# Transposes of an attention block moved from TensorE to VectorE and DMA, with the feed-forward stage moved into the next batch

## The chip, the cores and the metric

The kernel runs on one core of a Trainium2 chip. The metric is the device time of one execution in microseconds (us), as a median over timed runs. One further execution is recorded by the hardware profiler; the rows shown below come from it.

## The reference

Four batches of 1024 tokens with 512 channels, all in float32. Each batch has six vectors of modulation from a small condition. The attention has 16 heads, but the same scores for every head (`head_f` is all ones), and the feed-forward stage is a sum over eight square factors, so that both reduce to plain products.

```python
mod = (_silu(L0_c) @ L0_wmod).reshape(L0_c.shape[0], 6, 1, -1)
sa, ca, ga, sb, cb, gb = (mod[:, 0], ..., mod[:, 5])
ga = (2 * (ga >= 0) - 1) * jnp.maximum(jnp.abs(ga), 0.25)   # gb likewise
h = _layernorm(x, axis=-1) * (1 + ca) + sa
x = x + ga * attention(h, Wq, Wk, Wv, Wo)
h = _layernorm(x, axis=-1) * (1 + cb) + sb
x = x + gb * ffn(h, factors, bias)

# attention: qf = h @ Wq.T, kf = h @ Wk.T (rank 64)
scores = jnp.einsum('hr,bir,bjr->bhij', head_f, qf, kf)
attn = softmax(scores)
out = attn @ (h @ Wv.T) @ Wo.T          # heads side by side
# ffn: einsum('btd,rde->bte', x, factors) / sqrt(8) + bias
```

## The kernel before

A batch is held as eight tiles `x` of 128 tokens by 512 channels. TensorE contracts over partitions, so what is contracted has to stand with the contracted index on the partitions; that is what the transposes are for. A float32 product of 128x512 is two instructions in the profile.

The stages of a batch are these.

- **First normalization** (`ln1`, L312): statistics of each tile on VectorE, the inverse root by a power on POOL (`rstd_of`, L270), then `xn_a` on VectorE (`normalize`, L281), in two halves of four tiles.
- **Its transpose.** For batch 0 by TensorE (`hT_steps`). For the others by `hT_by_dma` (L326): VectorE transposes each tile in blocks of 32 by 32 into `st` (L335), and 16 SBUF to SBUF transfers per half, issued on the sync queue SP, carry the blocks to their places in `hT_a` (L338). Each moves 64 KB in runs of 512 bytes.
- **Projection** (`project`, L371) to queries and keys, one call per half.
- **Scores and softmax.** `scores(b, p)` (L398) takes a pair of token tiles: the products, the row maximum on VectorE (L417), the exponential on ScalarE (L419), which writes the numerators `pr` and their sums. `transpose_probs(b, p, jp)` (L425) transposes the numerators on TensorE, four 128x128 blocks to a PSUM tile (`ps_pt`, L433), and ScalarE and VectorE copy these by turns to `pt` (L440, L442). The denominators are applied later, in `attn_out`.
- **First product** (`z_steps(b, half)`, L450): `xn_a` transposed times `pt`, for a half of the tokens in eight steps, a column block of 128 channels in two steps; the result goes to `zt` by ScalarE and VectorE by turns (L466, L468).
- **Output product** (`attn_out`, L493): `zt` times the combined weight `w` of the batch (`make_w`); VectorE adds it to `x` (L502) and takes the statistics of the second normalization.
- **Second normalization** (`ln2`, L511): `xn_f`; then eight groups per batch of four TensorE transposes (`ln2_transposes`, `ps_hT_f`, L295), whose results are scaled and shifted to `hT_f` by ScalarE (L302) and VectorE (L306) by turns.
- **Feed-forward** (`ffn`, L529): `hT_f` times the summed factors `f` (`make_f`); VectorE adds it to `x` (L538), SP stores the tile (L539) and loads the tile of the batch after next into the same place (L99).

`sum_factors` (L251) adds the eight factors in batch 0's loop, through three staging buffers filled on SP.

The loop over `b` computes the first product of batch `b` while it prepares projection, scores and softmax of batch `nb = b + 1`. `weave(main, fill)` interleaves two lists of steps by hand. The order on each engine is fixed when the program is built: it follows the source, but an instruction whose operands or buffers are judged to be late is overtaken by later ones. On the chip each engine, and each DMA queue, works its list in order. PSUM has two tiles for scores, two for transposes (`ps_t`) and two for products (`ps_m`). The numerators of a pair and `xn_f` share two buffers (`prp`), `hT_a` and `hT_f` share two (`hp`).

Of the kernel before, what the change touches and what calls it, by code (L numbers as in the profile page):

```python
# [30 lines left out]
def kernel(  # L31
# [17 lines left out]
    nc = tc.nc  # L49
# [6 lines left out]
    GT = NT // 2  # L56
    GW = GT * P
    EPS = 1e-5
    PSUM = bass.MemoryType.PSUM
# [15 lines left out]
    ps_s = ctx.enter_context(tc.tile_pool(name="ps_s", bufs=2, space=PSUM))  # L75
    ps_t = ctx.enter_context(tc.tile_pool(name="ps_t", bufs=2, space=PSUM))
    ps_m = ctx.enter_context(tc.tile_pool(name="ps_m", bufs=2, space=PSUM))

    def psum_mm(name):
        return ps_m.tile([P, 512], F32, tag="mm", name=name)  # L80

    def psum_tr(name):
        return ps_t.tile([P, 512], F32, tag="tr", name=name)

# [92 lines left out]
    def channels(rows, name, plus):  # L177

        ps = psum_tr(f"ps_ch_{name}")
        for kc in range(KC):  # L180
            nc.tensor.transpose(ps[:, ts(kc, B)], rows[:, ts(kc, P)], ident[0:B, 0:B])
        m = const.tile([P, KC, B], F32, name=f"mod_{name}")
        nc.vector.tensor_scalar(
            m.rearrange("p k b -> p (k b)"), ps[:, : KC * B], plus, None, ALU.add
        )
        return m
# [26 lines left out]
    def first_rows():  # L213
# [3 lines left out]

        ps = psum_tr("ps_qbias")
        for kc in range(KC):
# [31 lines left out]
    def sum_factors():  # L251
        for kc in range(KC):
            acc = None
            for r in range(NR):
                f = stg.tile([P, D], F32, tag="stg", name=f"factor_{kc}_{r}")
                nc.sync.dma_start(out=f, in_=factors[r, ts(kc, P), :])
                if r > 0:
                    nc.vector.tensor_tensor(fsum[:, kc, :], acc, f, ALU.add)  # L258
                acc = f if r == 0 else fsum[:, kc, :]
# [18 lines left out]
    def normalize(b, tiles, mv, xn, name):  # L278
        r = rstd_of(mv, tiles, name)
        for j, t in enumerate(tiles):  # L280
            nc.vector.tensor_scalar(  # L281
                xn[:, j, :], xt[b, t], mv[:, t, 0:1], r[:, j : j + 1],
                ALU.subtract, ALU.mult,
            )
# [5 lines left out]
    def transpose_group(xn, hT, kc, name, scale=None, shift=None):  # L290


        ps = psum_tr(f"ps_hT_{name}_{kc}")
        for j in range(GT):
# [26 lines left out]
    def add_c1(b):  # L321
        bc = spread("c1", b)
        for t in range(NT):
            nc.vector.tensor_tensor(xt[b, t], xt[b, t], bc, ALU.add)

    def hT_by_dma(b, g):  # L326

        Q = 32
        st = stp.tile([P, KC, P // Q, GT, Q], F32, tag="st", name=f"st_a_{b}_{g}")
        hT = hp.tile([P, KC, GW], F32, tag="hT", name=f"hT_a_{b}_{g}")
        for t in range(GT):
            nc.vector.transpose(st[:, :, :, t, :], xn1[b, g][:, t, :])  # L335
        for k in range(P // Q):
            for c in range(P // Q):
                nc.sync.dma_start(  # L338
                    out=hT[ts(c, Q), :, ts(k, GT * Q)], in_=st[ts(k, Q), :, c, :, :]
                )  # L340
        return hT
# [50 lines left out]

    def qk_steps(b, hT):
        return [lambda g=g: project(b, g, hT[g]) for g in range(2)]

    probs, rinv, PT = {}, {}, {}

    def scores(b, p):  # L398
# [14 lines left out]
        den = small.tile([P, 2], F32, tag="den", name=f"den_{b}_{p}")  # L413
        pr2 = prp.tile([P, 2, T], F32, tag="pr", name=f"pr_{b}_{p}")
        for k, (i, ps) in enumerate(pss):
            nm = small.tile([P, 1], F32, tag="nm", name=f"nm_{b}_{i}")
            nc.vector.tensor_reduce(nm, ps, AX.X, ALU.max, negate=True)  # L417
            pr = pr2[:, k, :]
            nc.scalar.activation(  # L419
                pr, ps, AF.Exp, bias=nm, scale=1.0, accum_out=den[:, k : k + 1]  # L420
            )
            probs[b, i] = pr
        nc.vector.reciprocal(rinv[b][:, 2 * p : 2 * p + 2], den)

    def transpose_probs(b, p, jp):  # L425

        half, off = divmod(2 * p, GT)
        if (b, half) not in PT:
            PT[b, half] = ptp.tile([P, NT, GW], F32, tag="pt", name=f"pt_{b}_{half}")
        ps = psum_tr(f"ps_pt_{b}_{p}_{jp}")  # L430
        for jj in range(2):
            for k in range(2):
                nc.tensor.transpose(  # L433
                    ps[:, ds((2 * jj + k) * P, P)],
                    probs[b, 2 * p + k][:, ts(2 * jp + jj, P)], ident,
                )
        dst = PT[b, half][:, ts(jp, 2), ds(off * P, 2 * P)]
        src = ps.rearrange("p (j i) -> p j i", j=2)
        if jp % 2 == 0:
            nc.scalar.copy(dst, src)  # L440
        else:
            nc.vector.tensor_copy(dst, src)  # L442

    def softmax_steps(b, p, nxt):
        steps = [] if nxt is None else [lambda: scores(b, nxt)]
        return steps + [lambda jp=jp: transpose_probs(b, p, jp) for jp in range(NT // 2)]

    ZT = {}

    def z_steps(b, half):  # L450
# [5 lines left out]
        def part(dc, jh):  # L456
# [7 lines left out]
            if jh == 1:  # L464
                if dc % 2 == 0:
                    nc.scalar.copy(zt[:, dc, :], hold[dc])  # L466
                else:
                    nc.vector.tensor_copy(zt[:, dc, :], hold[dc])  # L468

# [40 lines left out]

    def ln2(b, g):  # L511
        if g == 0:
            bias_b[b] = spread("gbias", b)
        xn = prp.tile([P, GT, D], F32, tag="pr", name=f"xn_f_{b}_{g}")
        xn2[b, g] = normalize(b, halves(g), mv2[b], xn, f"f_{b}_{g}")
        hT2[b, g] = hp.tile([P, KC, GW], F32, tag="hT", name=f"hT_f_{b}_{g}")
        for t in halves(g):
            nc.vector.tensor_tensor(xt[b, t], xt[b, t], bias_b[b], ALU.add)  # L518
# [40 lines left out]
    scores(0, 0)  # L559
    for p in range(NT // 2):  # L560
        for step in softmax_steps(0, p, p + 1 if p + 1 < NT // 2 else None):
            step()
        if p == 0:
            second_rows()
    add_c1(0)
    make_w(0)


    for b in range(B):
        nb = b + 1 if b + 1 < B else None  # L570
        if nb is not None:
            hTn = []
            for g in range(2):
                ln1(nb, g)
                hTn.append(hT_by_dma(nb, g))
            scale_wqk(nb)
        weave(z_steps(b, 0), [] if nb is None else qk_steps(nb, hTn))
        if nb is not None:
            add_c1(nb)
            scores(nb, 0)  # L580
        if b == 0:
            sum_factors()
        make_f(b)
        weave(
            z_steps(b, 1),
            [] if nb is None else softmax_steps(nb, 0, 1) + softmax_steps(nb, 1, 2),
        )
        fill = [] if nb is None else softmax_steps(nb, 2, 3) + softmax_steps(nb, 3, None)
        weave([lambda t=t: attn_out(b, t) for t in halves(0)], fill[:5])
        ln2(b, 0)  # L590
        weave(
            [lambda t=t: attn_out(b, t) for t in halves(1)],
            fill[5:] + ln2_transposes(b, 0),
        )
        if nb is not None:
            make_w(nb)
        ln2(b, 1)
        weave([lambda t=t: ffn(b, t) for t in halves(0)], ln2_transposes(b, 1))
        for t in halves(1):
            ffn(b, t)  # L600

# [32 lines left out]
```

## Time and profile before

| | |
|---|---|
| timed runs | 620.51, 625.64 (median) and 627.34 us |
| profiled execution | 620.23 us, span of its instructions 618.2 us, mean granted TensorE clock 0.992 |
| TensorE, busy | 591.9 us (96%) |
| VectorE, busy | 321.9 us (52%) |
| ScalarE, busy | 93.6 us (15%) |
| POOL, busy | 16.8 us (3%) |
| SP queue | 44.37 MB, 22.7% of the 16 DMA engines' span |
| transposes of numerators, L433 | 256 instructions |
| transposes of the second normalization, L295 | 128 instructions |

The span runs from the first to the last instruction; the profiled execution's own time adds 2.0 us around it. PE is TensorE's matrix multiply, PEld its weight load, DVE VectorE, ACT ScalarE, SPq the sync queue. In a row of the lines view, the operation is followed by the tile it writes and those it reads, their shapes and the count; then the busy time in us and the mean of one in ns; then the idle time of the engine before them and what ended it. Matmuls overlap one another, so that a mean of one is longer than the distance from one to the next.

### The profile page before, as it was taken

Reading aid. Unit: us, or ns where it says so; the run is one execution under the profiler, and the core shown is the slowest. Engines: PE = TensorE matmul, PEld = TensorE weight load, DVE = VectorE, ACT = ScalarE, POOL = GpSimd, SP = SyncE. Lnnn points to the kernel's source line nnn. Section 1 sums busy time; section 2 is a strip of 40 time slices with the busy share of each in tenths; the row PEclk is TensorE's granted clock in tenths of the full one; section 3 lists DMA queues with packets and bytes.
Section 4 is the critical chain, followed back from the end, with each engine's and each line's share of the span. In section 5 each row is a group of like instructions: output and inputs, shape, how many; then the busy total and the mean of one; then the engine's idle time right before and its main releaser. Section 6 shows DMA issues by size and latency. Waiting matters only on the chain.

```text
span 618.2 us, 4783 instructions
## 1 busy us (share of the span) xinstructions
PE 591.9 (96%) x1744; PEld 272.2 (44%) x1744; DVE 321.9 (52%) x586; ACT 93.6 (15%) x154; POOL 16.8 (3%) x22
## 2 busy tenths in 40 slices
PE   6898949999999999999999999999999999999997
PEld 3343514344455444344454444344454444444443
DVE  5459993775578584332578584222578220005651
ACT  0223401222211001222211001222211000000110
POOL 1000000000000000000000000000000000000000
PEclk9999988999999999999999999999999999999999
DMA  8950135553001453000001453000001200000011
GB/s 310 381 193 0 37 102 138 186 170 103 0 0 51 154 161 91 21 0 1 0 0 52 154 160 99 12 0 1 0 1 35 101 35 0 1 0 1 0 68 69
DMA packets 35391, 44.67 MB, mean 72 GB/s; under 512 B 4116, under 2 KB 16916, under 8 KB 35368
## 3 DMA queue, kind: packets, MB, share of 16 engines
q1 hardware_dynamic: 35368, 44.37, 22.7%
q8 instruction: 14, 0.23, 0.2%
q14 instruction: 9, 0.07, 0.0%
HBM read 29.64 MB, written 8.42 MB: 62 GB/s over the span
## 4 chain that ended last, share of the span: by engine, by line
PE 80%; DVE 14%; SPq 2%; POOL 2%; issue 1%; DMA 1%; ACT 0%; POOLq 0%; ACTq 0%
PE ps_z L460 34%; PE ps_f L533 14%; PE ps_o L497 14%; PE ps_sc L408 5%; PE ps_qk L371 5%; PE ps_pt L433 3%; DVE xn_f L281 2%; PE ps_hT_f L295 2%; DVE w L481 2%; SPq L338 1%; DVE x L502 1%; DVE x L518 1%; POOL r_f L270 1%; DVE bn_a L275 1%; DVE xn_a L281 1%
## 5 line engine op out<-in xcount | busy, mean ns | idle before, releaser
L460 PE MATMUL ps_z<-pt,xn_a 128*128 128x512 f32 x512 | 227.2, 595 | 0.0
L460 PEld LDWEIGHTS ps_z<-pt,xn_a 128*128 128x128 f32 x512 | 94.7, 190 | 116.2 <-issue 114.0
L497 PE MATMUL ps_o<-w,zt 128*128 128x512 f32 x256 | 114.9, 594 | 0.0
L533 PE MATMUL ps_f<-f,hT_f 128*128 128x512 f32 x256 | 113.3, 592 | 0.0
L533 PEld LDWEIGHTS ps_f<-f,hT_f 128*128 128x128 f32 x256 | 47.2, 191 | 51.5 <-issue 50.0
L497 PEld LDWEIGHTS ps_o<-w,zt 128*128 128x128 f32 x256 | 46.5, 190 | 50.4 <-issue 48.1
L468 DVE COPY zt<-ps_z 128x512 f32<-128x512 f32 x16 | 11.0, 689 | 90.2 <-PE ps_z L460 90.2
L419 ACT ACTIVATE pr<-ps_sc,nm 128x1024 f32<-128x1024 f32 x32 | 35.5, 1113 | 72.0 <-DVE nm L417 72.0
L417 DVE TENSOR_REDUCE nm<-ps_sc 128x1 f32<-128x1024 f32 x32 | 37.8, 1213 | 16.2 <-PE ps_sc L408 16.2
L502 DVE SCALAR_TENSOR_TENSOR x<-ps_o,ri,x 128x512 f32<-128x512 f32 x32 | 23.9, 746 | 41.9 <-PE ps_o L497 41.6
L538 DVE TENSOR_TENSOR x<-ps_f,x 128x512 f32<-128x512 f32 x32 | 21.9, 685 | 40.8 <-PE ps_f L533 40.8
L408 PE MATMUL ps_sc<-kT,qT 64*128 64x512 f32 x128 | 41.1, 617 | 1.6 <-ACT pr L419 1.6
L433 PEld LDWEIGHTS ps_pt<-ident,pr 128*128 128x128 f32 x256 | 30.0, 141 | 27.4 <-issue 18.5
L371 PE MATMUL ps_qk<-hT_a,wqk 128*128 128x512 f32 x64 | 30.3, 621 | 9.9 <-DMA hT_a<-st_a 9.4
L433 PE MATMUL ps_pt<-ident,pr 128*128 128x128 f32 x256 | 36.2, 275 | 1.5 <-ACT pt L440 1.0
L442 DVE COPY pt<-ps_pt 128x512 f32<-128x512 f32 x32 | 21.8, 682 | 21.1 <-PE ps_pt L433 21.0
L440 ACT COPY pt<-ps_pt 128x512 f32<-128x512 f32 x32 | 18.8, 587 | 88.0 <-PE ps_pt L433 87.9
L466 ACT COPY zt<-ps_z 128x512 f32<-128x512 f32 x16 | 9.4, 586 | 131.6 <-PE ps_z L460 131.6
L302 ACT ACTIVATE hT_f<-ps_hT_f,mod_sb,mod_cb 128x512 f32<-128x512 f32 x16 | 12.5, 779 | 103.9 <-PE ps_hT_f L295 88.5
L258 DVE TENSOR_TENSOR fsum<-fsum,factor 128x512 f32<-128x512 f32 x24 | 16.5, 688 | 16.8 <-DMA factor<-in_factors_dram 16.5
L275 DVE BATCH_NORM_STATS2 bn_a<-x 128x6 f32<-128x512 f32 x32 | 21.2, 672 | 7.4 <-DMA x<-in_x_dram 7.4
L408 PEld LDWEIGHTS ps_sc<-kT,qT 64*128 64x128 f32 x128 | 13.8, 186 | 25.1 <-issue 19.4
(82 smaller groups left out, 334.0 us busy)
## 6 DMA issues: line engine op xcount, KB each, us to landing
x<-in_x_dram SPq DMA_DIRECT2D x32, 256.0 KB, 4.1
factor<-in_factors_dram SPq DMA_DIRECT2D x32, 256.0 KB, 3.0
out_dram<-x SPq DMA_DIRECT2D x32, 256.0 KB, 2.0
hT_a<-st_a SPq DMA_DIRECT2D x96, 64.0 KB, 2.0
wm_a<-in_wmod_dram SPq DMA_DIRECT2D x2, 1024.0 KB, 9.5
wm_b<-in_wmod_dram SPq DMA_DIRECT2D x2, 1024.0 KB
wvs<-in_wv_dram SPq DMA_DIRECT2D x4, 256.0 KB
wos<-in_woT_dram SPq DMA_DIRECT2D x4, 256.0 KB, 4.8
```

The lines of the kernel that those rows point to most:

```text
L275: nc.vector.bn_stats(st, src)
L371: nc.tensor.matmul(ps[: 2 * R, :], wqkb[b][:, kc, :], hT[:, kc, :], start=(kc == 0), stop=(kc == KC - 1),)
L408: nc.tensor.matmul(ps[:, ts(h, 512)], qT[h * R : (h + 1) * R, ts(i, P)], kT[h * R : (h + 1) * R, :], start=True, stop=True,)
L417: nc.vector.tensor_reduce(nm, ps, AX.X, ALU.max, negate=True)
L419: nc.scalar.activation(pr, ps, AF.Exp, bias=nm, scale=1.0, accum_out=den[:, k : k + 1])
L433: nc.tensor.transpose(ps[:, ds((2 * jj + k) * P, P)], probs[b, 2 * p + k][:, ts(2 * jp + jj, P)], ident,)
L442: nc.vector.tensor_copy(dst, src)
L460: nc.tensor.matmul(hold[dc], xn1[b, jh][:, j - jh * GT, ts(dc, P)], PT[b, half][:, j, :], start=(j == 0), stop=(j == NT - 1),)
L497: nc.tensor.matmul(ps, ZT[b, half][:, kc, ts(j, P)], wb[b][:, kc, :], start=(kc == 0), stop=(kc == KC - 1),)
L502: nc.vector.scalar_tensor_tensor(xi, ps, rinv[b][:, t : t + 1], xi, ALU.mult, ALU.add)
L533: nc.tensor.matmul(ps, hT2[b, g][:, kc, ts(j, P)], fb[b][:, kc, :], start=(kc == 0), stop=(kc == KC - 1),)
L538: nc.vector.tensor_tensor(xi, ps, xi, ALU.add)
```

## The change

The numerators are transposed by VectorE, in place, in blocks of 32 by 32: one instruction for a pair. The exponential writes them in a layout in which the blocks that go to the same partitions stand together, and `move_blocks` then issues 16 SBUF to SBUF transfers per pair on SP, in runs of 64 numbers (256 bytes). Only pairs 0 and 1 of batch 0 are still transposed by TensorE, and ScalarE makes all copies of these. The tokens of `pt` are then in another order, which the copy to `zt` undoes; all of these copies are on ScalarE.

The second normalization is transposed in the same way, except in the last batch: one VectorE instruction and 16 transfers per half, in runs of 32 numbers (128 bytes). ScalarE then scales and shifts `hT_f` in place.

`ffn` of a batch moves to the next loop, after the first two steps of that batch's first product, and the first normalization of the batch after comes behind it. The projection moves from the first half of the first product to the second, with the softmax pairs 0 to 2; pair 3 goes to `attn_out`. The weight `w` is made in the loop that uses it. PSUM keeps two tiles for scores and has four for products and transposes together. All but the first three factor loads go from SP to POOL's queue.

The diff, cut to its core:

```diff
-    ps_t = ctx.enter_context(tc.tile_pool(name="ps_t", bufs=2, space=PSUM))
-    ps_m = ctx.enter_context(tc.tile_pool(name="ps_m", bufs=2, space=PSUM))
+    ps_m = ctx.enter_context(tc.tile_pool(name="ps_m", bufs=4, space=PSUM))
...
             for r in range(NR):
-                nc.sync.dma_start(out=f, in_=factors[r, ts(kc, P), :])
+                queue = nc.sync if kc == 0 and r < 3 else nc.gpsimd
+                queue.dma_start(out=f, in_=factors[r, ts(kc, P), :])
...
+    def move_blocks(src, dst, width):
+        for r in range(NQ):
+            for c in range(NQ):
+                nc.sync.dma_start(
+                    out=dst[ts(c, Q), :, ts(r, width)], in_=src[ts(r, Q), :, c]
+                )
...
+    def by_dma(b, half):
+        return (b, half) != (0, 0)
...
-        pr2 = prp.tile([P, 2, T], F32, tag="pr", name=f"pr_{b}_{p}")
+        pr2 = prp.tile([P, 2 * T], F32, tag="pr", name=f"pr_{b}_{p}")
+        if by_dma(b, 2 * p // GT):
+            view = pr2.rearrange("p (c k e) -> p k c e", k=2, e=Q)
+        else:
+            view = pr2.rearrange("p (k j) -> p k j", k=2)
...
-    def transpose_probs(b, p, jp):
+    def transpose_probs(b, p):
         half, off = divmod(2 * p, GT)
+        pr2 = probs[b, p][0]
+        nc.vector.transpose(pr2, pr2)
+        move_blocks(
+            pr2.rearrange("p (j c w) -> p j c w", j=NT, c=NQ),
+            pt_tile(b, half)[:, :, ds(off * P, 2 * P)], 2 * Q,
+        )
...
+    def softmax(b, p):
+        scores(b, p)
+        transpose_probs(b, p)
...
             if jh == 1:
-                if dc % 2 == 0:
-                    nc.scalar.copy(zt[:, dc, :], hold[dc])
-                else:
-                    nc.vector.tensor_copy(zt[:, dc, :], hold[dc])
+                dst, src = zt[:, dc, :], hold[dc]
+                if by_dma(b, half):
+                    dst = dst.rearrange("p (h t r a) -> p h r t a", h=2, t=2, r=NQ)
+                    src = src.rearrange("p (h r t a) -> p h r t a", h=2, t=2, r=NQ)
+                nc.scalar.copy(dst, src)
...
     def ln2(b, g):
...
+        if b + 1 == B:
+            xn2[b, g] = normalize(
+                b, halves(g), mv2[b], xn.rearrange("p (t d) -> p t d", t=GT), f"f_{b}_{g}"
+            )
+        else:
+            normalize(
+                b, halves(g), mv2[b],
+                xn.rearrange("p (k t e) -> p t k e", k=KC, t=GT), f"f_{b}_{g}",
+            )
+            nc.vector.transpose(xn, xn)
+            src = xn.rearrange("p (n c a) -> p c n a", c=NQ, a=Q)
+            dst = hT2[b, g].rearrange("p k (t r a) -> p r (k t) a", t=GT, r=NQ)
+            for r in range(NQ):
+                for c in range(NQ):
+                    nc.sync.dma_start(out=dst[ts(c, Q), r], in_=src[ts(r, Q), c])
+            for kc in range(KC):
+                hc = hT2[b, g][:, kc, :]
+                nc.scalar.activation(
+                    hc, hc, AF.Identity, bias=second["sb"][:, kc, b : b + 1],
+                    scale=second["cb1"][:, kc, b : b + 1],
+                )
...
-    for p in range(NT // 2):
-        for step in softmax_steps(0, p, p + 1 if p + 1 < NT // 2 else None):
-            step()
-        if p == 0:
-            second_rows()
-    add_c1(0)
-    make_w(0)
+    scores(0, 1)
+    for jp in range(NT // 2):
+        transpose_probs_pe(0, 0, jp)
+    second_rows()
+    softmax(0, 2)
+    for jp in range(NT // 2):
+        transpose_probs_pe(0, 1, jp)
+    softmax(0, 3)
     for b in range(B):
         nb = b + 1 if b + 1 < B else None
+        z0 = z_steps(b, 0)
+        for step in z0[:2]:
+            step()
+        if b > 0:
+            for t in range(NT):
+                ffn(b - 1, t)
+        hTn = []
         if nb is not None:
-            hTn = []
             for g in range(2):
                 ln1(nb, g)
                 hTn.append(hT_by_dma(nb, g))
             scale_wqk(nb)
-        weave(z_steps(b, 0), [] if nb is None else qk_steps(nb, hTn))
+        for step in z0[2:]:
+            step()
+        add_c1(b)
+        make_w(b)
+        fill = []
         if nb is not None:
-            add_c1(nb)
-            scores(nb, 0)
+            fill = [lambda g=g: project(nb, g, hTn[g]) for g in range(2)]
+            fill += [lambda p=p: softmax(nb, p) for p in range(3)]
+        weave(z_steps(b, 1), fill)
         if b == 0:
             sum_factors()
         make_f(b)
         weave(
-            z_steps(b, 1),
-            [] if nb is None else softmax_steps(nb, 0, 1) + softmax_steps(nb, 1, 2),
-        )
-        fill = [] if nb is None else softmax_steps(nb, 2, 3) + softmax_steps(nb, 3, None)
-        weave([lambda t=t: attn_out(b, t) for t in halves(0)], fill[:5])
+            [lambda t=t: attn_out(b, t) for t in halves(0)],
+            [] if nb is None else [lambda: softmax(nb, 3)],
+        )
         ln2(b, 0)
         weave(
             [lambda t=t: attn_out(b, t) for t in halves(1)],
-            fill[5:] + ln2_transposes(b, 0),
-        )
-        if nb is not None:
-            make_w(nb)
+            ln2_transposes(b, 0) if nb is None else [],
+        )
         ln2(b, 1)
-        weave([lambda t=t: ffn(b, t) for t in halves(0)], ln2_transposes(b, 1))
-        for t in halves(1):
-            ffn(b, t)
+    b = B - 1
+    weave([lambda t=t: ffn(b, t) for t in halves(0)], ln2_transposes(b, 1))
+    for t in halves(1):
+        ffn(b, t)
```

## The prediction

> **What bounds the kernel now.** I read first the busy table and the slices, then one whole loop, then the TensorE timeline inside it, then the sync queue (SP) that would carry the new transfers.
>
> ```profile
> PE 591.9 (96%) x1744; PEld 272.2 (44%) x1744; DVE 321.9 (52%) x586; ACT 93.6 (15%) x154; POOL 16.8 (3%) x22
> ...
> PE   6898949999999999999999999999999999999997
> ```
>
> TensorE works 96% of the span; the gaps lie in the first six slices. So only work taken off TensorE, or those gaps, can pay. One loop of steady state, from one `ps_f` run to the next:
>
> ```profile
> 206.90 13.74 PE ps_f L533 x32
> 220.64 13.73 PE ps_z L460 x32
> ...
> 345.81 13.74 PE ps_f L533 x32
> ```
>
> The period is 345.81 − 206.90 = 138.91 us. Its products cost, by the same chain: 128 of `ps_z` at 13.73 per 32, 54.9; 64 of `ps_o` and 64 of `ps_f` at 3.44 per 8, 27.5 each; two projections 2 x 3.43; four score pairs 4 x 1.92. Sum 124.5. The other 14.4 us are 24 groups of four transposes (16 `ps_pt`, 8 `ps_hT_f`): 0.60 us a group, which the timeline bears out (0.43 for the four, the rest at the changes between kinds):
>
> ```profile
> 285.61 0.60 PE L433 MATMUL ps_pt<-ident,pr 128*128 128x128 f32 x4
> 286.05 3.60 PE L460 MATMUL ps_z<-pt,xn_a 128*128 128x512 f32 x8
> ```
>
> **What goes.** In each of three loops all 24 groups leave TensorE: 43.2 us, less 0.8 a loop for the handovers at the scores that stay: **−40.8**. Ahead of the loops, pairs 2 and 3 of batch 0 lose 8 groups, about 0.5 each: **−4**. The last batch keeps its eight `ps_hT_f` groups. And one large wait loses its place:
>
> ```profile
> L371 PE MATMUL ps_qk<-hT_a,wqk 128*128 128x512 f32 x64 | 30.3, 621 | 9.9 <-DMA hT_a<-st_a 9.4 <-DVE wqk L355 0.5
> ```
>
> These 9.4 us fall in loop 0, where the projection of batch 1 stood after four steps of the first product. It now stands after ten, 20.6 us later: **−9.4**. But SP has 32 new transfers of batch 0 ahead of these; at the rate worked out below the second group lands about 2 us after TensorE asks: **+2**. Without any new wait the sum against the profiled execution is 620.2 − 40.8 − 4 − 9.4 + 2 = 568.
>
> **What VectorE and ScalarE take over.** The block transpose exists already:
>
> ```profile
> 235.54 2.48 DVE L335 STREAM_TRANSPOSE st_a<-xn_a 128x512 f32<-128x512 f32 x4
> ```
>
> A pair of numerators or a half of `xn_f` is four times this tile: 2.5 us, six times a loop, +15. Off VectorE go eight `pt` copies at 0.62, four `hT_f` evictions at 0.75 and four `zt` copies at 0.62: −10.5. Net +4.5 of 74 in a period of 139: hidden under TensorE. ScalarE loses eight copies and gains four `zt` copies and four more scalings, on 22 us of work in 139: hidden too. These costs count only as latency: scores end, the second maximum and exponential follow (reciprocal 2.8 us after the scores, L423 after L408), the transpose 2.5 more; about 5.7 with waits.
>
> **What SP gets, the heart of it.** A pair costs 16 transfers of 64 KB in runs of 256 bytes, a half of the second normalization 16 of 64 KB in runs of 128 bytes. Per loop that is 64 + 32, on top of 32 for `hT_a`. The nearest row is those 32, with runs of 512 bytes:
>
> ```profile
> L338 SPq DMA_DIRECT2D hT_a<-st_a x96: 585/599/1207, 81.2 to 386.3; - x96
> ...
> DMA to landing us min/median/max: 2.0/2.0/3.2
> ```
>
> ```profile
> 238.16 11.27 SPq L338 DMA_DIRECT2D hT_a<-st_a  x16
> ```
>
> One issue takes 0.60 us of the queue, with its gap 0.65; sixteen take 10.4. Loads of 256 KB take 0.33 to 0.34. Does the price grow with the number of runs? Bounds: 0.36 an issue (the load row and a gap) and, in proportion to runs, 1.3 for a pair's and 2.6 for a half's. Against growth stands that `wqk` and `wm_a`, whose sources have four runs a partition (512 in all), are issued in 0.37 and 0.38, hardly above the 0.33 of 128 runs. I take 0.65 for both, and keep a linear price as a rival. The engines behind the queue have room: in the window of the sixteen above their share was 0.37, which is 0.37 x 11.0 / 16 = 0.25 us for one transfer of 8 runs and a completion per engine, 28 ns a run; 17 or 33 records, if none took less, would be 0.48 or 0.92 us. The first lies below the issue, the second above it, by 0.27, or 16 x 0.27 = 4.3 us a half; shorter runs should take less than 28 ns, so I leave it at the issue.
>
> **Where a loop now waits.** Clock from the start of `z_steps(b, 1)`. Pair 0's scores end at 5 x 3.44 + 2 x 3.43 + 1.92 = 26.0, its transposed block is ready at 31.7. From there SP is nearly continuous: pairs 0, 1, 2, 3, then the first half of the second normalization (`ln2(b, 0)`), its row spreads (0.8), then the second half. The last of the first half lands 1.45 after its issue ends, one scaling takes 0.78, semaphores 0.4. TensorE asks for that half (`ffn(b, 0)`) after product, projections, scores, `attn_out` and two steps of the next first product: 27.5 + 6.9 + 7.7 + 27.5 + 6.9 = 76.4. With c1 for a pair's issue and c2 for a half's, the wait is 31.7 + 0.8 + 64 c1 + 16 c2 + 2.6 − 76.4 = 64 c1 + 16 c2 − 41.3. At 0.65 that is **10.7 us a loop**, if TensorE keeps to the source's order. The second half is issued by 10.4 later, while four `ffn` tiles cover 13.8: no wait.
>
> The source's order is not kept where an operand is late:
>
> ```profile
> 254.90 1.98 PE L408 MATMUL ps_sc<-kT,qT 64*128 64x512 f32 x4
> 256.81 1.12 PE L460 MATMUL ps_z<-pt,xn_a 128*128 128x512 f32 x2
> 257.87 1.98 PE L408 MATMUL ps_sc<-kT,qT 64*128 64x512 f32 x4
> ```
>
> Two `ps_z` are put between the scores of one pair while `kT` is copied. Likewise I expect one more column block of `ps_z` (two steps, 6.9 us) ahead of `ffn(b, 0)`; the PSUM pool, now four buffers, still holds the last `attn_out` tiles, so not more. Against this: in loop 0 the projection waited 9.4 us with `ps_z` behind it. I take 10.7 − 6.9 = about **4 us a loop, +12**, with 0 and 10.7 as its ends.
>
> **Edits at nothing, and their cover.** Exponentials of pair 2 wait for the landing of pair 0 (two `pr` buffers): ScalarE stands about 2 us, TensorE has 13.8 us of `attn_out` meanwhile. `ln2(b, 0)`'s normalizations wait likewise for pair 2's landing; behind them on VectorE stand the `attn_out` evictions of tiles 4 to 7, and so the PSUM buffer of the next `ps_z`: up to 3 us of TensorE, inside the wait above. Stores and loads of `ffn` queue behind the second half's transfers, then `hT_a`: they land some 10 us before the projection asks; without that cover every us counts. The three scalings per half that follow the first run faster than TensorE's four products. Factor loads on POOL: 29 issues, which no row shows; between SP's 0.33 and the 1.01 of a power (L270) they are 10 to 29 us of POOL in loop 0, and a power queued behind one that waits for a VectorE sum could hold `hT_a` a few us; the summed factors are wanted only a loop later. I take 0, up to 5.
>
> **A rule against it.** The Trainium skill, "DMA: Bandwidth & Descriptors", Specifications, says transfers of under 512 bytes a descriptor fall below line rate, since the engine reads, modifies and writes. No row here has a short run written from SBUF to SBUF. If each run cost twice the 28 ns above, an issue would be 0.95 and 1.85 us, the wait 64 x 0.95 + 16 x 1.85 − 41.3 = 49 us, and the kernel above 700. The same page ("Why small descriptors are slow (HBM only)") takes SBUF to SBUF out of the penalty for small packets; by that the sum stays as it is.
>
> **Sum.** 568 + 12 = 580 in the terms of the profiled execution. The three timed runs (620.51 to 627.34) have their median 5.4 us above it; I add 5 for a median: **585**. About 1% is what a measurement of this kernel can tell from no change.
>
> **Rivals.**
> Everything hidden (chance 0.17): products enough are put ahead of `ffn`. For it: the `ps_z` rows above; against: the 9.4 us. 568 + 5 = 573.
> Source order, full wait (0.18): 568 + 3 x 10.7 + 5 = 605; with SP's price at 0.70 some 10 us more, 615.
> SP becomes the bound (0.28, the other side): an issue's price grows with the runs in a partition. Load row 0.33, `hT_a` with 4 runs 0.60: 0.0675 a run gives 0.87 for 8 and 1.41 for 16, with gaps 0.92 and 1.46. The first half then waits 64 x 0.92 + 16 x 1.46 − 41.3 = 41, the second 23.4 − 13.8 = 9.6: 50.6 x 3 = 152, so 725; at half that growth 0.79 and 1.06: 26 and 3 a loop, 660. It decides from where 3 waits eat 620 − 568: 17.5 a loop, 0.73 an issue for both. For it: 0.60 against 0.33 is unexplained. Against: `wqk` and `wm_a`.
>
> **Chances and range.** Forecast (573 to 600) 0.32; hidden 0.17; full wait 0.18, of which 0.03 ends within 1%; SP bound 0.28, of which 0.02 within 1%; another mishap of a few tens of us, as in the softmax pairs, 0.05, of which 0.03 within 1% and 0.02 slower. Faster 0.64, same 0.08, slower 0.28. Range 565 to 645, the likeliest case alone 573 to 600.
>
> **What would show it.** Right: no `ps_pt` row but 32 transposes, `ps_hT_f` only in the last batch, periods near 128, SP issues of 0.6 us back to back for some 60 us a loop, the wait of `ps_f` for DMA or ScalarE at 0 to 11 us a loop, the projection's wait near 2. Wrong: issues above 0.73, waits of `ps_z` for `pt` or `ps_sc` for `pr`, or VectorE late in the `attn_out` stage.

## The result and the profile after

The change makes the kernel slower. Its median is 674.3 us (671.8 to 676.7, four runs) against 625.7 (620.5 to 627.3) for the kernel before on the same chip: a ratio of 1.079, 95% interval 1.072 to 1.087. The profiled execution took 676.7 us, its span 674.9. It is the slowest of its four runs, and the profiled execution before (620.2) lies below all four of its own, so the two profiles differ by 56.5 us and the medians by 48.6. From the page, the busy table, TensorE's busy slices and the clock granted to it:

```profile
PE 566.4 (84%) x1424; PEld 244.8 (36%) x1424; DVE 328.5 (49%) x546; ACT 97.2 (14%) x158; POOL 34.6 (5%) x51
...
PE   6989989429992399999992399999991499999997
...
PEclk9988999858996599999997599999996699999999
```

TensorE lost its 320 transposes and 25.5 us of busy time, but its share fell from 96% to 84%. Its slices have four holes, and the clock is low in each. Three holes stand once a loop, ahead of `ps_f`; the first stands in loop 0. The chain that ended last gives the period (start, duration, what):

```profile
229.97 30.65 PE ps_f L582 x64
...
381.50 29.99 PE ps_f L582 x64
```

381.50 − 229.97 = 151.5 us, where 138.9 stood before. The groups of the page name the waits (after the second bar: idle time before the group, and what ended it):

```profile
L582 PE MATMUL ps_f<-f,hT_f 128*128 128x512 f32 x256 | 118.5, 623 | 70.3 <-DMA hT_f<-xn_f 47.2
...
L421 PE MATMUL ps_sc<-kT,qT 64*128 64x512 f32 x128 | 40.8, 675 | 23.4 <-ACT kT L396 21.8
```

The feed-forward waits 70.3 us in three loops, 23.4 each, for its transposed normalization. The scores wait 21.8 us for the keys, all but 0.3 of it in loop 0.

**SyncE's price is what was forecast.** For each line on the queue: issues, then minimum, median and maximum of one in ns:

```profile
L334 SPq DMA_DIRECT2D pt<-pr x224: 585/609/1726, 74.0 to 518.7; - x112
...
L559 SPq DMA_DIRECT2D hT_f<-xn_f x96: 585/627/649, 216.4 to 540.2; - x96
```

0.61 and 0.63 us with 8 and 16 runs a partition, against 0.60 with 4: at this size it does not grow with the runs. But the queue is not continuous. Its timeline in loop 1:

```profile
312.46 55.93 SPq L334 DMA_DIRECT2D pt<-pr  x64
368.49 21.43 SPq L559 DMA_DIRECT2D hT_f<-xn_f  x32
```

64 issues at 0.65 are 41.6 us; these took 55.9. SyncE stood some 14 us for VectorE. The last exponentials of pairs 2 and 3 on ScalarE's timeline, and then VectorE's, show why (in brackets the idle time before an instruction):

```profile
326.58 1.11 ACT L439 ACTIVATE pr<-ps_sc,nm 128x1024 f32<-128x1024 f32 x1
...
342.39 1.10 ACT L439 ACTIVATE pr<-ps_sc,nm 128x1024 f32<-128x1024 f32 x1
```

```profile
335.68 0.75 DVE L529 SCALAR_TENSOR_TENSOR x<-ps_o,ri,x 128x512 f32<-128x512 f32 x1 [1.74 <-PE ps_o L524]
...
337.78 2.31 DVE L448 STREAM_TRANSPOSE pr<-pr 128x2048 f32<-128x2048 f32 x1
...
355.64 2.29 DVE L448 STREAM_TRANSPOSE pr<-pr 128x2048 f32<-128x2048 f32 x1
...
369.98 1.91 DVE L284 TENSOR_SCALAR xn_f<-x,mv,r_f 128x512 f32<-128x512 f32 x4 [5.65 <-DMA pt<-pr]
```

The exponentials of pair 2 end at 327.7, yet its transpose comes at 337.8: on VectorE it stands behind four additions of `attn_out`, each of which waits 1.7 us for TensorE. Pair 3's stands behind the other four and the weight `w`, 12 us after its exponential. The second half of the second normalization waits 5.65 us for a landing, since `xn_f` shares the two `pr` buffers. TensorE's timeline at the end of this:

```profile
351.32 7.03 PE L485 MATMUL ps_z<-pt,xn_a 128*128 128x512 f32 x16
381.50 8.96 PE L582 MATMUL ps_f<-f,hT_f 128*128 128x512 f32 x15 [23.14 <-ACT hT_f L562]
```

One column block of `ps_z`, then 23 us of nothing: the source's order, with no further block put ahead.

**Loop 0.** The first eviction of the queries, on VectorE, stands behind the additions of the factors, most of which wait for their load:

```profile
109.41 0.69 DVE L258 TENSOR_TENSOR fsum<-fsum,factor 128x512 f32<-128x512 f32 x1 [0.80 <-DMA factor<-in_factors_dram]
...
137.72 0.74 DVE L392 TENSOR_SCALAR qT<-ps_qk,qbias 64x512 f32<-64x512 f32 x1
```

28 additions run from 87 to 138 us. ScalarE's part of the eviction, and the keys' (L396) behind it, wait for VectorE's:

```profile
138.49 0.68 ACT L393 ACTIVATE qT<-ps_qk,qbias 64x512 f32<-64x512 f32 x1 [29.52 <-DVE qT L392]
```

The second eviction comes at 146.8, since VectorE makes `w` and `f` between the two. The projection had ended by 122.1, and TensorE's scores stand:

```profile
139.92 2.07 PE L421 MATMUL ps_sc<-kT,qT 64*128 64x512 f32 x2 [14.41 <-ACT kT L396]
149.00 3.78 PE L421 MATMUL ps_sc<-kT,qT 64*128 64x512 f32 x6 [7.01 <-ACT kT L396]
```

### The profile page after: what moved, and what is told of

It is laid out like the page before. It is cut to its first block, busy times and chain, and to the rows that moved or that the text cites. A ratio compares the mean times of both kernels' runs of the same rounds, so it can differ in the third digit from the quotient of the medians.

```text
span 674.9 us, 4570 instructions
## 1 busy us (share of the span) xinstructions
PE 566.4 (84%) x1424; PEld 244.8 (36%) x1424; DVE 328.5 (49%) x546; ACT 97.2 (14%) x158; POOL 34.6 (5%) x51
## 3 DMA queue, kind: packets, MB, share of 16 engines
q1 hardware_dynamic: 142808, 57.75, 33.4%
## 4 chain that ended last, share of the span: by engine, by line
PE 69%; DVE 10%; SPq 9%; DMA 7%; issue 3%; ACT 1%; POOL 1%; DVEq 0%; POOLq 0%; ACTq 0%
PE ps_z L485 23%; PE ps_f L582 17%; PE ps_o L524 16%; DMA factor<-in_factors_dram 5%; SPq L559 5%; SPq L334 4%; PE ps_sc L421 4%; PE ps_qk L378 3%; PE ps_wvo L152 2%; DVE pr L448 2%; DVE w L508 1%; DMA hT_f<-xn_f 1%; DVE nm L436 1%; DVE fsum L258 1%; PE ps_c L234 1%
## 5 line engine op out<-in xcount | busy, mean ns | idle before, releaser
L582 PE MATMUL ps_f<-f,hT_f 128*128 128x512 f32 x256 | 118.5, 623 | 70.3 <-DMA hT_f<-xn_f 47.2
L485 PEld LDWEIGHTS ps_z<-pt,xn_a 128*128 128x128 f32 x512 | 97.5, 192 | 128.9 <-issue 127.4
L582 PEld LDWEIGHTS ps_f<-f,hT_f 128*128 128x128 f32 x256 | 50.6, 201 | 134.4 <-ACT hT_f L562 74.4
L421 PE MATMUL ps_sc<-kT,qT 64*128 64x512 f32 x128 | 40.8, 675 | 23.4 <-ACT kT L396 21.8
L495 ACT COPY zt<-ps_z 128x512 f32<-128x512 f32 x32 | 18.7, 585 | 237.3 <-PE ps_z L485 237.3
L448 DVE STREAM_TRANSPOSE pr<-pr 128x2048 f32<-128x2048 f32 x14 | 32.2, 2298 | 0.6
L562 ACT ACTIVATE hT_f<-hT_f,mod_sb,mod_cb 128x512 f32<-128x512 f32 x24 | 17.6, 802 | 89.4 <-DMA hT_f<-xn_f 89.4
L392 DVE TENSOR_SCALAR qT<-ps_qk,qbias 64x512 f32<-64x512 f32 x8 | 5.9, 741 | 47.4 <-PE ps_qk L378 47.4
L270 POOL TENSOR_TENSOR r_f<-v_f,mhalf 128x4 f32<-128x4 f32 x8 | 9.2, 1147 | 357.2 <-DVE v_f L266 183.8
L284 DVE TENSOR_SCALAR xn_f<-x,mv,r_f 128x512 f32<-128x512 f32 x32 | 15.2, 539 | 20.0 <-DMA pt<-pr 17.6
L275 DVE BATCH_NORM_STATS2 bn_f<-x 128x6 f32<-128x512 f32 x32 | 22.2, 693 | 0.9
```

Source lines behind the costliest of these rows:

```text
L275: nc.vector.bn_stats(st, src)
L421: nc.tensor.matmul(ps[:, ts(h, 512)], qT[h * R : (h + 1) * R, ts(i, P)], kT[h * R : (h + 1) * R, :], start=True, stop=True,)
L448: nc.vector.transpose(pr2, pr2)
L485: nc.tensor.matmul(hold[dc], xn1[b, jh][:, j - jh * GT, ts(dc, P)], PT[b, half][:, j, :], start=(j == 0), stop=(j == NT - 1),)
L582: nc.tensor.matmul(ps, hT2[b, g][:, kc, ts(j, P)], fb[b][:, kc, :], start=(kc == 0), stop=(kc == KC - 1),)
```

## The experiments

Where a ratio is given, the time is a median and the ratio is to the kernel before on the same chip; the others are single runs. The theory to begin with: the 23.4 us a loop are the queue's part that the prediction's formula gives (about 10) and the rest VectorE's late transposes; loop 0's wait is the factors' additions. The rivals: SyncE's queue alone, or the short runs in the DMA engines.

**1. No sum over factors.** One load per chunk takes the place of eight loads and seven additions.

```diff
-            for r in range(NR):
-                f = stg.tile([P, D], F32, tag="stg", name=f"factor_{kc}_{r}")
...
+            nc.gpsimd.dma_start(out=fsum[:, kc, :], in_=factors[0, ts(kc, P), :])
```

> Leaves out the sum over the factors: each block of f comes from one factor, loaded straight into place, so that VectorE has no sums and no waits for their loads (small tiles have two buffers instead of four, which the next kernel needs). Theory: in loop 0 the projection's eviction stood behind these sums, and TensorE waited 14.4 + 7.0 us for the keys; this goes, with some 5 us of slow clock after it: 676.7 - 26 = about 650, the wait of the feed-forward stage stays at 23 us a loop. Rival, POOL and the loads only share the time with another wait (transfers of pairs): the keys come late all the same, and the time stays above 665.

646.7 us, 30 less than the changed kernel's profiled run, and the scores wait 2.1 us in all, at most 0.4 of it for the keys. The feed-forward's wait stays: 69.9 us over three loops. So loop 0's loss belongs to the factors, and the rest does not.

**2. A third buffer for `pr` and `xn_f`,** on top of 1.

```diff
-    prp = ctx.enter_context(tc.tile_pool(name="prp", bufs=2))
+    prp = ctx.enter_context(tc.tile_pool(name="prp", bufs=3))
```

> The kernel of e1 with a third buffer for the numerators (same part left out). Pairs 2 and 3 no longer wait for a buffer, and their block transposes stand ahead of the additions of the output product on VectorE. Theory: of the 23 us that the feed-forward stage waits in each loop, some 12 come from these late transposes and 11 from 80 issues in a row on the SP queue; so 23 becomes about 11, and the time 650 - 3 x 13 = about 612. Rival, SP alone (its price or the engines behind it): the wait stays at 20 us or more, 640 to 650. Rival, the second normalization's own path is too long: no change either.

622.7 us; the wait falls from 23.3 to 15.1 a loop, not to 11. The queue is now nearly continuous in the pairs, and has a gap behind them:

```profile
274.07 43.08 SPq L326 DMA_DIRECT2D pt<-pr  x64
321.94 21.44 SPq L551 DMA_DIRECT2D hT_f<-xn_f  x32
```

From 317.15 to 321.94 SyncE has nothing to issue: the first half's normalization starts at 317.18 on VectorE, behind additions. So 8.2 us a loop were the late pairs, 4.8 are the late normalization, and 10.3 are left, near the 10.7 of the formula.

**3. All pairs by TensorE,** the second normalization still by DMA.

```diff
     def by_dma(b, half):
-        return (b, half) != (0, 0)
+        return False
...
-        transpose_probs(b, p)
+        for jp in range(NT // 2):
+            transpose_probs_pe(b, p, jp)
```

> The numerators of all pairs go back to TensorE, the second normalization stays with VectorE and SP. Theory: with no pairs ahead of it on SP the second normalization lands about when it is asked for: waits of 0 to 5 us a loop, a period of 124.7 + 16 x 0.6 + 2 = 136 to 139 and, with loop 0's wait still there, 625 to 640. Rival, its own path (block transpose, 16 issues, landing, scaling) is too long: the wait stays above 10 us a loop, period over 145, 655 or more.

633.6 us, ratio 1.015 (1.011 to 1.018). The feed-forward waits 9.2 us in the whole kernel, 3.1 a loop: the normalization's transfers, the ones with the shortest runs, cost little when no pair is queued ahead of them. The transposes are back on TensorE and wait 21.6 us for ScalarE's exponentials, since nothing is woven between them. Loop 0's wait, which was expected to stay, is gone: the scores wait 2.0 us in all, though the additions are on VectorE and their loads on POOL as in the changed kernel. That the time fell into the expected range is in part luck, two errors of some 20 us each that cancel. VectorE's timeline has the first addition 17 us earlier than in the changed kernel, and the first eviction of the queries ahead of the last addition:

```profile
69.99 0.67 DVE L258 TENSOR_TENSOR fsum<-factor,factor 128x512 f32<-128x512 f32 x1
...
123.53 0.73 DVE L392 TENSOR_SCALAR qT<-ps_qk,qbias 64x512 f32<-64x512 f32 x1
```

**4. The second normalization by TensorE,** the pairs by DMA.

```diff
-        if b + 1 == B:
+        if True:
             xn2[b, g] = normalize(
...
-            ln2_transposes(b, 0) if nb is None else [],
+            ln2_transposes(b, 0),
```

> The second normalization goes back to TensorE, the numerators of the pairs stay with VectorE and SP, the feed-forward stage stays where the change put it. Theory: nothing then waits for SP in steady state: a period of 124.7 + 0.7 + 8 x 0.6 = 130, so 3 x 21 less and 2 us a loop of slow clock less: about 610, with loop 0's wait of some 21 us still there. Rival, the pairs' transfers are late for the first product too: waits of ps_z for pt of over 5 us a loop, 625 or more.

650.2 us, ratio 1.041 (1.034 to 1.048): a miss by 40. The wait did not go away, it moved to the transposes of that normalization, which wait 36.1 us for `xn_f`, 12 a loop:

```profile
342.92 1.92 DVE L284 TENSOR_SCALAR xn_f<-x,mv,r_f 128x512 f32<-128x512 f32 x4 [5.68 <-DMA pt<-pr]
...
343.52 0.47 PE L297 MATMUL ps_hT_f<-ident,xn_f 128*128 128x128 f32 x1 [11.53 <-DVE xn_f L284]
```

`xn_f` needs one of the two buffers that the pairs hold until they land, and the pairs' issues run from 303.3 to 351.8. Loop 0's wait is there too. The changed kernel has the same two buffers, so its first half cannot be normalized before pair 2 has landed either.

**5. The factors' additions on POOL.**

```diff
-                    nc.vector.tensor_tensor(fsum[:, kc, :], acc, f, ALU.add)
+                    nc.gpsimd.tensor_tensor(fsum[:, kc, :], acc, f, ALU.add)
```

> The 28 additions of the factors are made by POOL instead of VectorE; everything is computed. Theory: loop 0's wait comes from VectorE's order (the projection's eviction stands behind additions that wait for loads), not from the loads, the POOL queue or the transfers of pairs; so the keys' wait of 21 us and the slow clock after it go, as where the sum was left out: 645 to 652. Rival, the loads themselves or POOL's queue are too slow for loop 0: the wait moves to the feed-forward weights or stays, 665 or more.

651.4 us, ratio 1.046 (1.031 to 1.061). The scores wait 2.6 us in all, the feed-forward 70.3 as before. The loads are on POOL here as well, so their new queue alone does not make loop 0's wait; with 1 and 3, this shows that the additions' place on VectorE does. Whether they would end sooner with their loads on SP was not run.

**6. The feed-forward two steps later.**

```diff
-        for step in z0[:2]:
+        for step in z0[:4]:
```

(and `z0[4:]` behind it.)

> The feed-forward stage comes after four steps of the next first product instead of two. Theory: nothing before it gets later, so its wait of 23 us a loop falls by the 6.9 us of two steps, to 16, with the projection still covered: 676 - 3 x 7 = about 655. Rival, the first normalization behind it becomes late (waits of the projection for hT_a of 5 us or more a loop): 665 to 677.

662.5 us, ratio 1.064 (1.053 to 1.074). The wait falls from 23.1–23.7 to 16.4–17.0, by one column block of 6.8, so the order is the source's. The span falls by 14.5, not 21: the period is 146.5 to 147.2, and the projection now waits 0.5 us a loop for its own transfers, which come behind the feed-forward. What takes the other 1 to 2 us a loop was not traced further.

**7. All pairs by TensorE, woven.** As in 3, but the scores of the next pair are placed ahead of each pair's transposes, the copies are shared by ScalarE and VectorE, and pairs 2 and 3 spread over `attn_out`, as in the kernel before.

```diff
-            fill += [lambda p=p: softmax(nb, p) for p in range(3)]
+            fill += [lambda: scores(nb, 0)]
+            fill += softmax_steps(nb, 0, 1) + softmax_steps(nb, 1, 2)
...
+        tail = [] if nb is None else softmax_steps(nb, 2, 3) + softmax_steps(nb, 3, None)
```

> The numerators of all pairs by TensorE with the scores of the next pair ahead of a pair's transposes, as in the kernel before; the second normalization by VectorE and SP, the feed-forward stage inside the next first product. Theory: against e3 (633) the transposes no longer wait for their exponentials, 6 us a loop, and 4 in front: about 612, that is 2% under the kernel before, with a wait of the feed-forward stage of 1 to 4 us a loop. Rival, the second normalization's path of some 20 us has no slack once TensorE is faster: its wait grows to 8 us a loop, 625.

621.1 us, ratio 0.995 (0.990 to 1.000). What 3 lost to ScalarE comes back (the transposes wait 1.9 us in all). The periods, from one second half of `ps_f` to the next, are 137.2 and 137.7 us: eight groups of transposes at 0.6 fewer than before, and up to two waits of 1.4 at the feed-forward. The time is 9 above the 612 expected: in loop 0 the scores wait 6.4 us (4.6 for an addition of the factors, 1.9 for the keys). That half of the change can be had almost without a wait, but by itself it is worth little.

**8. Pairs 0 and 1 by DMA, pairs 2 and 3 by TensorE,** batch 0 by TensorE, the additions on POOL.

```diff
     def by_dma(b, half):
-        return False
+        return b > 0 and half == 0
```

> As e7, but pairs 0 and 1 of batches 1 to 3 by VectorE and SP, pairs 2 and 3 by TensorE; factors summed by POOL. Theory: SP has 32 issues of pairs, done 21 us after the first, well ahead of the second normalization, so its wait stays under 5 us a loop, and eight groups a loop are saved against e7: 612 - 3 x 8 x 0.6 = about 598, if loop 0 is no worse. Rival, the two buffers for numerators and xn_f hold the later pairs back as in the changed kernel: waits of ps_pt or ps_sc of over 5 us a loop, 615 or more.

616.4 us, ratio 0.990 (0.977 to 1.002), 18 above what was expected. The feed-forward's wait is 4.9 us a loop, and the first product starts at 83.4, where its unbroken run starts at 73.8 in the kernel before. VectorE is slow while POOL adds. Its timeline:

```profile
97.01 8.14 DVE L326 TENSOR_TENSOR x<-x,bc_c 128x512 f32<-128x512 f32 x8
```

The same eight additions took 4.89 us in the kernel before.

**9. A quarter of the issues.**

```diff
-            for r in range(NQ):
-                for c in range(NQ):
-                    nc.sync.dma_start(out=dst[ts(c, Q), r], in_=src[ts(r, Q), c])
+            for c in range(NQ):
+                nc.sync.dma_start(out=dst[:, c], in_=src[:, c])
```

(The pairs' transfers likewise.)

> The changed kernel with each block transpose's transfer issued as 4 transfers of four times the runs in place of 16: the same bytes in runs of the same length, a quarter of SyncE's instructions. Each block keeps its partitions, so what is transferred isn't the transpose; the amount of work is otherwise the same. If the price is SyncE's for each issue (0.65 us pitch whatever the issue holds), the queue's 52 us + 21 us a loop fall to about 13 + 5, the feed-forward's wait of 23 us a loop loses the queue's part (10 us) and about 16 us of issuing behind the second normalization, and 0 to 9 us a loop are left, which VectorE's late transposes set; time 600 to 635. If the price lies in the engines that move the short runs (a busy share of 0.58 while the normalization's transfers run, 0.41 while the numerators' do), the pitch of an issue grows to about four times, the wait stays at 20 us or more and the time stays above 660.

579.5 us in its one run, below the range given; the feed-forward had been expected to wait up to 9 us a loop for VectorE. From the chain:

```profile
187.07 27.47 PE ps_f L585 x64
...
312.27 27.47 PE ps_f L585 x64
```

The feed-forward waits for nothing. The period is 125.2 us, 0.7 above the prediction's sum of products. The engines carry the same runs, so they are not the limit. But VectorE's order changed too: pair 2's transpose now stands ahead of all of `attn_out`'s additions, pair 3's and the first half's normalization ahead of the second four, and loop 0's wait is 8.6 us. So the run does not part SyncE's price from VectorE's order. An issue of 256 KB takes a median of 0.68 us with 8 runs a partition and 1.15 with 16, not four times 0.6; the shortest of either took 0.59. At this size the median does grow with the runs, and what sets it was not traced.

**10 and 11. The kernel of 8 with the additions back on VectorE; then the feed-forward behind `z0[:4]`.**

> The kernel of the run with pairs 0 and 1 of batches 1 to 3 moved by DMA and the rest by TensorE, with the additions of the factors back on VectorE. The theory is that POOL's additions slowed VectorE's work in front (8.14 us for eight rows that took 4.89 before) and held back the first batch by some 12 us, and that on VectorE they cost the 4 to 6 us of wait at the first key eviction that the woven run showed: 616.4 - 12 + 6 = about 610, range 602 to 614, first product of the numerators back before 75 us. The rival, that the front is late because of the first batch's own transposes by TensorE and not POOL, gives 618 to 624 with that product still near 83 us.

> The same, with the feed-forward put behind four column blocks of the next batch's first product in place of two. The feed-forward's wait of 4.8 us a loop lies beside 6.8 us of products and goes, and with it the lower clock behind it (about 1 to 2.5 us a loop): 3 x 6 to 7 = 18 to 22 us less than the run beside it, about 590 (583 to 600). Rival: the projection's normalization and its transfers come behind the feed-forward's accumulation on VectorE and then the projection waits, as much as the feed-forward did: 605 to 612.

10: 616.2 us, ratio 0.988 (0.982 to 0.994), no better than 8. The theory's first half held: the first product starts at 73.1, and VectorE's timeline has the eight additions at their old length:

```profile
78.75 4.90 DVE L326 TENSOR_TENSOR x<-x,bc_c 128x512 f32<-128x512 f32 x8
```

Its price did not: the scores in loop 0 wait 7.1 us and then run at a lower clock, which gives back the 10 us; the first `ps_f` starts at 199.1, and at 197.6 in 8. 11: 605.0 us, ratio 0.970 (0.964 to 0.976): 11 less, not 18 to 22. The feed-forward's wait fell to 1.4 a loop; the projection's transfers now come late, as the rival had it (3.0 us in all), and loop 0 waits as before.

**12. As many issues, one run a partition.** The numerators are written so that the 512 numbers for one group of partitions lie together; the same for `xn_f`, which lands in `st` and is put in order by ScalarE's scaling. In both kernels a transfer moves 64 KB.

```diff
-            view = pr2.rearrange("p (c k e) -> p k c e", k=2, e=Q)
+            view = pr2.rearrange("p (c j k e) -> p k j c e", c=NQ, k=2, e=Q)
...
+    def move_rows(src, dst):
+        for r in range(NQ):
+            for c in range(NQ):
+                nc.sync.dma_start(out=dst[ts(c, Q), r], in_=src[ts(r, Q), c])
```

> The changed kernel with the numerators and the second normalization laid out so that each of the 16 transfers of a block transpose reads one run of 2 KB from each of its 32 partitions and writes one run of 2 KB (the numerators' rows are then read by TensorE in pieces of 64 columns; the normalization lands in the buffer that the projection's transpose uses, and ScalarE's scaling puts it in order). The number of issues is as in the changed kernel, 96 a loop, and the same bytes move. If the price of an issue falls with the runs (the loads of a whole tile, one run a partition, take 0.33 to 0.38 us), SyncE's work on a loop falls from 63 to some 35 us, the feed-forward's wait from 23 us to 0 to 3, and the time is 580 to 592. If an issue of 32 partitions costs 0.65 whatever its runs are, the queue's part of the wait (10 us and the slow clock behind it) stays: 579 (the run with a quarter of the issues) + 3 x 13 = about 618, range 605 to 650.

618.5 us, ratio 0.993 (0.990 to 0.997), on the second of the two values. The issue's price is a median of 0.59 us with one run of 2 KB: it belongs to the issue. VectorE's order changed here too: pair 2's transpose stands behind one addition of `attn_out`, pair 3's behind four, the first half's normalization behind six. The queue has no gap up to the end of the first half. SyncE's timeline, and TensorE's:

```profile
281.06 41.83 SPq L341 DMA_DIRECT2D pt<-pr  x64
322.98 10.03 SPq L341 DMA_DIRECT2D st_f<-xn_f  x16
```

```profile
335.34 4.97 PE L597 MATMUL ps_f<-f,hT_f 128*128 128x512 f32 x6 [8.38 <-ACT hT_f L576]
```

64 x 0.65 = 41.6, and a wait of 8.4 to 9.6 us: this is the prediction's formula (10.7) with nothing in its way.

**13. The same with the feed-forward behind `z0[:4]`.**

> The same, with the feed-forward put behind four column blocks of the next batch's first product in place of two. With the price near 0.35 there is no wait left to hide and the time is the same within 1%: 576 to 592. With the price at 0.65, 6.8 of 10 us a loop are hidden: 590 to 605.

598.1 us, ratio 0.961 (0.955 to 0.967): the best version that computes everything, faster than both kernels. The feed-forward waits 7.8 us in three loops. In loop 1 it is what is left of 8.4 after 6.8 us of products:

```profile
328.69 11.86 PE L597 MATMUL ps_f<-f,hT_f 128*128 128x512 f32 x27 [1.56 <-ACT hT_f L576]
```

## Why the prediction was wrong

By its own steps, in the terms of the profiled execution (620.2 before, 568 without a new wait, 580 with it, 676.7 measured):

| step | predicted | measured | from |
|---|---|---|---|
| transposes leave TensorE, three loops | −40.8 | −41.1 | (138.9 − 125.2) x 3, run 9 |
| front of batch 0 | −4 | +1.5 | start of `ps_z` less what ran ahead of it: 70.3 before, 71.8 after |
| projection's wait in loop 0 | −9.4 | −9.4 | no such wait after |
| transfers ahead of `hT_a` | +2 | +1.7 | one wait of `ps_z` |
| feed-forward's wait | +12 | +70.3 | L582 |
| clock behind it | none | +7.7 | 30.65 + 29.99 + 29.47 − 3 x 27.47 |
| factors in loop 0 | 0, up to 5 | +26 | 14.4 + 7.0, and about 4.8 of slow clock: 3.78 and 9.37 for scores and `ps_z` that take 1.44 and 6.87 elsewhere |

The measured column adds to 56.7 and the change took 56.5. **Right** were what TensorE would gain, the price of an issue (0.65 with its gap, whatever the runs), VectorE's 2.5 us for a block transpose (2.30), and the queue's part: 10.3 us are left in run 2, 8.4 to 9.6 in run 12. That shorter runs take the engines less than 28 ns was right as well: their share was 0.58 while the 32 transfers of loop 1's normalization ran, which is at most 0.58 x 21.41 / 32 = 0.39 us a transfer and not 0.92. Four steps failed.

First, "I expect one more column block of `ps_z` (two steps, 6.9 us) ahead of `ffn(b, 0)`". The order stayed the source's; runs 6 and 13 put that block ahead by hand and got the 6.8 us. The rival of the full wait had this right, and with it 10.7 us in place of 4.

Second, and larger, "Edits at nothing, and their cover". The text named both waits, pair 2's exponential for a landing and `xn_f` for another, but set them "inside the wait above". It followed the additions that stand behind a late normalization, and not the transposes and the normalization that stand behind the additions. VectorE works in the order that was fixed when the program was built, and there pairs 2 and 3 come behind four and eight additions paced by TensorE. Each us by which a transpose is late is a us for which SyncE stands, and SyncE's queue is the chain to the feed-forward. Run 2 puts 8.2 us a loop on the pairs and 4.8 on the normalization. "VectorE late in the `attn_out` stage" was on the list of what would show the prediction wrong; it was given 0.05 together with other mishaps and "a few tens of us", and it cost 39 without the clock.

Third, "the summed factors are wanted only a loop later. I take 0, up to 5". They are, but the additions stand in VectorE's list ahead of the queries' eviction, and most of them wait for a load. The prediction looked at POOL's queue for what stands behind a wait and not at VectorE's. Runs 1 and 5, which take the additions off VectorE, both remove the loss, and run 3 removes it with the additions still there, in another order.

Fourth, the clock was left out. It cost 7.7 us behind the feed-forward's wait. Without it, and without the front, which came out 5.5 above its term for a reason that was not traced, the error would be 13 us smaller.

The rival that ended slower, SyncE as the bound by a price that grows with the runs, came out at a time near the measured one (660 to 725) with a mechanism that the changed kernel's own issues (0.61 and 0.63) and run 12 exclude. Its slope was also taken wrongly: from one run at 0.33 to four at 0.60 are three runs and not four, 0.09 a run and not 0.0675, so by its own rule it should have stood higher still. On the Trainium skill's rule for transfers of under 512 bytes ("DMA: Bandwidth & Descriptors", Specifications): the engines do pay, but little, about 11%. The same 57.75 MB took 33.4% of 674.9 us of the sixteen engines in the changed kernel and 32.9% of 614.6 in run 12, 225 against 202 us, and neither is the limit.

What stays open: why an issue of 64 KB between SBUF partitions costs 0.6 us of the queue and a load of 256 KB 0.33 to 0.38. For issues of 64 KB the number of runs a partition is excluded. Sixteen blocks in four issues were tried only in the form of run 9, in which each block keeps its partitions.

## What to carry to other kernels

When work is moved to a queue that feeds the critical engine, write down the order in which the engine that fills this queue gets its instructions, and ask of each what it waits for; a cheap instruction behind one that is paced by the critical engine is late by that engine's pace. A shared buffer pool ties the stages that use it together: here a third buffer took 8.2 us a loop off the wait, and a layout that changed the order on VectorE 14.4, against some 10 for the price of the transfers. Where a wait cannot be removed, move independent products ahead of it by hand and look whether what comes behind them is then late.

## What the hardware showed that was not expected

TensorE's granted clock falls in a wait, and the work behind the wait pays for it. In the stretch from 206 to 230 us of the changed kernel, with TensorE idle, the granted clock is 0.55, and the 64 `ps_f` that follow take 30.65 us in place of 27.47. Waits of 4.7 to 5.0 us do the same (29.98 to 30.36 in run 10), waits of 1.4 do not (27.73 in run 11). Between them run 13 has one that did not and a shorter one that did (the first 32 `ps_f` of one loop, and the 64 of another):

```profile
198.75 14.00 PE L597 MATMUL ps_f<-f,hT_f 128*128 128x512 f32 x32 [2.62 <-ACT hT_f L576]
...
459.56 29.43 PE L597 MATMUL ps_f<-f,hT_f 128*128 128x512 f32 x64 [2.53 <-ACT hT_f L576]
```

In the 10.4 us behind the second the granted clock is 0.84, behind the first it is 1.00. The Trainium skill, "TensorE: Matmul & The Clock Gate" (Part 1, "What's actually happening"), has the gate close after an idle window of about 3.4 us that runs freely. The waits of 1.4 us and of 4.7 us and more agree with it; the one of 2.53 us is shorter than that window and was followed by a lower clock all the same.

VectorE slows down beside POOL's additions. Runs 8 and 10 differ in the source only by the engine that adds the factors: eight additions of a row to `x` took 8.14 and 4.90 us, four products for `w` 7.74 and 2.73. The Trainium skill, "SBUF — State Buffer" (SBUF: two separate sides), says that a VectorE instruction with two SBUF inputs and a POOL instruction that reads SBUF exclude each other on a shared pair of ports; both of these have two such inputs, POOL's additions read SBUF, and the rows agree. Moving these additions to POOL was therefore not free for VectorE.
